# Two fused image blocks on one core: background work placed behind the even decay, finer steps for TensorE, and the first projection in two halves

## The chip, the cores and the metric

The kernel runs on one core of a Trainium2 chip. The metric is the device time of one execution in microseconds; the lower it is, the better. A time is the median of several runs; the profile is of one further execution.

The engines are TensorE (PE in the profile, its weight loads PEld), VectorE (DVE), ScalarE (ACT), GpSimd (POOL) and SyncE (SP), which issues all the DMAs of this kernel. Each engine works off its own list of instructions in order, and waits at an instruction until what that needs is there. SBUF is the memory that all of them work in, PSUM the smaller one that PE writes to; ACT and DVE use both.

## The reference

All arrays are float32. There are 16 images of 64 x 64 positions with 96 channels, and two layers, each added to its input (x + layer(norm(x))), where the norm is over groups of 3 channels of one image.

Layer 0 enlarges an image by Fourier interpolation, applies 96 -> 384 channels, a quadratic function, 384 -> 96 channels, a low-pass filter, and takes every second position. Layer 1 is a selective scan in four directions over the 4096 positions:

```python
xz = einsum('bhwc,pc->bhwp', x, in_proj_w);  xc, z = xz[..., :192], silu(xz[..., 192:])
xc = silu(depthwise_conv3x3(xc) + conv_b)              # 192 channels
xs = 4 orders of xc: by rows, by columns, and both reversed
dts, Bs, Cs = split(einsum('bkdl,kcd->bkcl', xs, x_proj_weight))     # 6, 16, 16
delta = softplus(einsum('bkrl,kdr->bkdl', dts, dt_projs_weight) + bias)
for t:  h = exp(delta_t * A) * h + (delta_t * u_t) * B_t;   y_t = sum_n h * C_t
y = sum of the four directions, put back in order;  layernorm over 192;  * z;  out_proj
```

For each image, direction, channel (192) and state (16) there is thus one recurrence over 4096 steps.

## The kernel before, in words

**Three kinds of work.** `front(mi)` (L240 to L517) makes of image mi the scan's inputs: layer 0, the second norm, the 3x3 convolution as nine matmuls ("taps", L482) and the gate z; it stores them to DRAM by rows (L473, L474) and, through the tile `col`, by columns (L508, L513). `scan()` (L615 on) does the recurrences of all images. `finish(mi)` (L519 to L608) adds the directions, applies norm, gate and output matrix, and stores the image. front and finish are generators: at each `yield` they hand back control, so that their instructions can be written into the scan's list in small steps. `front(0)` runs ahead of the scan, and `finish` of the last image behind it (L953 to L964).

**The scan.** An image has 8 steps (two pairs of directions, four stretches of T = 1024 positions each), a step has 6 blocks of 64 channel rows, a block 4 *units* of four states; 16 x 8 x 6 x 4 = 3072 units. Ahead of a step, `project` (L633 to L698) computes delta and delta * u ("dtu") for its 1024 positions in two halves of TB = 512, for three groups of channels each: a matmul (L666), six ACT instructions that make the softplus's parts e, m, w, d (L674 to L681), four matmuls with the identity that add them up (L686), a product on DVE (L691) and a copy on ACT (L692), and two stores to DRAM. The very first projection has nothing beside it (L738); the others are spread over the step before.

A unit has an odd half (e = 1) and an even half (e = 0), each of 128 partitions by 1024 positions. The loop L872 writes, in this order:

- `recur(n, 1)`: the odd scan on DVE (L770 or, backwards, L772), `keep` of its last value (L778), and ACT's `decay(n + 1, 1)`: exp(delta * A) for the next unit, L755. In every fifth unit (SHARE) the product with C follows on DVE (L906)
- `slot(0)`: the first background position
- POOL's product of the odd half with C (L915, not in every fifth unit), and `drive(n + 2)`: dtu * B, on POOL (L761)
- `recur(n, 0)`: the even scan on DVE; `read_out(n - 1)`: 16 matmuls (L794) that sum over the states
- `slot(1)`: the second background position (L923)
- the even half's product with C on DVE (L924), `keep` on ACT (L778), `decay(n + 1, 0)` on ACT (L755), and, once in a block, the copy of its result (L805)
- `slot(2)`: the third background position (L931); then loads of what comes: delta (L703), B and C rows (L722).

The decays write into the PSUM pool `sc_aps` (L629), which has two places of two banks each; the tile is called `da`. The odd scan reads its da and writes into the tile `b`; in every fifth unit, and always for the even half, the scan writes over da, and the product with C reads that. The program is written under a manual schedule (L953): the order on each engine is that of the code. Which of a pool's free places a tile gets is settled when the program is built.

**Background positions.** `slot` (L852) gives a step to the projection of the next step (`step_gen`, PSLICES = 71 steps over 72 positions), and one to `front` of the next image or, when that is through, to `finish` of the last one. An image has POS = 576 positions; a `Background` (L822) advances while its counted steps are behind SLICES / POS of the positions. A plain `yield` counts 1, `yield HEAVY` counts 2, and after `yield WAIT` the generator goes on only at a third position (L832).

**Memories.** Tiles of front and finish come from `b2p` (11 pieces of 128 x 512, L184), and from `b16` and `b18`, one large place each (L182, L183). In the scan the 8 PSUM banks are split into two for front and finish (`b_ps`), four for the decays, one for y and one for the projection (`gps`, L628 to L631).

Of the kernel before, what the change touches and what calls it, by code (L numbers as in the profile page):

```python
# [54 lines left out]
UPS = 100  # L55
# [16 lines left out]
SLICES = 550  # L72
# [7 lines left out]
def tile_two_blocks(  # L80
# [159 lines left out]
    def front(mi):  # L240
# [71 lines left out]
        o_last = None  # L312
        for p0 in range(0, UPS, PP):

            t1 = b18.tile([HW, PP, C], F32, name="t1", tag="b18")
            xr = fetch_x(0)
            for _ in range(3):
                yield
            for cg in range(3):
                u_ps = [bank([HW, 16, PP], "u_ps") for _ in range(2)]  # L320
                for k in range(16):
                    for a in range(2):
                        on = slice(64 * a, 64 * a + 64)
                        nc.tensor.matmul(
                            u_ps[a][:, k, :], lhsT=xr[k // 8][on, k % 8, :], rhs=up_s[on, p0:p0 + PP],
                            start=True, stop=True,
                        )
                    if k == 7:
                        yield
                if cg < 2:  # L330
                    xr = fetch_x(cg + 1)
                yield
                for a in range(2):
                    c0 = 48 * a + 16 * cg
                    nc.scalar.copy(t1[:, :, c0:c0 + 16], u_ps[a].rearrange("w c p -> w p c"))
                    yield
# [4 lines left out]
            for g in range(PP // PG):  # L341
# [8 lines left out]
                for j in range(HB + 1):  # L350
# [10 lines left out]
                    if j == 2 and sd is not None:  # L361
                        stow(sd, row - 2 * PG)
                    if j < HB:
                        h_ps[j] = bank([128, PG * UPS], "h_ps")
                        nc.tensor.matmul(  # L365
                            h_ps[j], lhsT=w1t_s[:, 128 * j:128 * (j + 1)],
                            rhs=xu.rearrange("c p q -> c (p q)"), start=True, stop=True,
                        )
                    elif g < PP // PG - 1:
                        xu_ps = widen(t1, g + 1)  # L370
# [90 lines left out]
        for i, n, tiles, both in ((0, 128, 8, 0), (1, 64, 4, 4)):  # L461
# [14 lines left out]
            for t in range(tiles):  # L476
                c_ps = bank([128, 8, HW], "c_ps")
                for tap in range(9):
# [8 lines left out]
                    if tap == 2 and turned is not None:  # L487
                        turn(*turned)
                    if tap % 3 == 2 and tap < 8:
                        yield HEAVY  # L490
# [13 lines left out]
                yield HEAVY  # L504
# [14 lines left out]
    def finish(mi):  # L519
# [19 lines left out]
        for t in range(8):  # L539
# [7 lines left out]
            for ob, n in ((0, 128), (1, 64)):  # L547
                oc = slice(128 * ob, 128 * ob + n)
                y_ps = bank([n, 8, HW], "yc")
                for i, (w, of) in enumerate(((pmat_s[:, 0, oc], y0), (pd_s[:, 0, oc], u0), (pd_s[:, 1, oc], yu))):  # L550
                    nc.tensor.matmul(  # L551
                        y_ps, lhsT=w, rhs=of.rearrange("c (h w) -> c h w", w=HW), start=(i == 0), stop=False
                    )
                if tail is not None:
                    tail = next(tail, None) and tail
# [3 lines left out]
                yield HEAVY  # L559
# [18 lines left out]
            yield HEAVY  # L578
# [5 lines left out]
            yield HEAVY  # L584
# [30 lines left out]
    def scan():  # L615


        with ExitStack() as es:
# [9 lines left out]
            banks.append(es.enter_context(tc.tile_pool(name="b_ps", bufs=2, space=PSUM)))  # L628
            aps = es.enter_context(tc.tile_pool(name="sc_aps", bufs=2, space=PSUM))  # L629
            yps = es.enter_context(tc.tile_pool(name="sc_yps", bufs=1, space=PSUM))  # L630
            gps = es.enter_context(tc.tile_pool(name="sc_gps", bufs=1, space=PSUM))  # L631

            def project(mi, pair, lc, out):  # L633
# [3 lines left out]
                out["rows"] = rows = dctx.tile([2, 2 * NS, T], F32, name="rows")  # L637
                out["delta"] = [dctx.tile([128, T], F32, name=f"delta_d{v}") for v in range(3)]
                out["dtu"] = [dctx.tile([128, T], F32, name=f"dtu_d{v}") for v in range(3)]
                xs_d = image[mi]["xs"]  # L640
                order = (0, 2, 1)

                def fetch_u(v, t):
                    uv = up_.tile([128, TB], F32, name="u")
# [3 lines left out]
                ahead_u = [fetch_u(v, 0) for v in order]  # L648
                for _ in range(4):
                    yield  # L650
                for t in range(0, T, TB):
                    u, ahead_u = dict(zip(order, ahead_u)), []
                    pp = gps.tile([128, TB], F32, name="pp", tag="g")
# [4 lines left out]
                    pr = pj.tile([128, TB], F32, name="pr")  # L658
# [3 lines left out]
                    for i, v in enumerate(order):  # L662
                        if i == 0:
                            yield
                        s = gps.tile([128, TB], F32, name="s", tag="g")
# [7 lines left out]
                        e, d, m, w = (pj.tile([128, TB], F32, name=k) for k in ("e", "d", "m", "w"))  # L673
# [9 lines left out]
                        s = gps.tile([128, TB], F32, name="s", tag="g")  # L683
# [3 lines left out]
                        for _ in range(3):  # L687
                            yield
                        dtu = pj.tile([128, TB], F32, name="dtu")
                        delta = pj.tile([128, TB], F32, name="delta")  # L690
# [6 lines left out]
                        if t + TB < T and i < 2:  # L697
                            ahead_u += [fetch_u(k, t + TB) for k in (order[:1], order[1:])[i]]  # L698
# [39 lines left out]
            for _ in project(*steps[0], ctxs[0]):  # L738
                pass
            bc = {(what, 0, j): fetch_bc(ctxs[0], 0, j, what) for j in range(NQ) for what in range(2)}  # L740
            dtus = {0: fetch_dtu(ctxs[0], 0)}
            deltas = {(0, e): fetch_delta(ctxs[0], 0, e) for e in (1, 0)}
# [114 lines left out]
            def next_step(st, mi):  # L857

                nonlocal step_gen
                if st < len(steps):  # L860
                    if steps[st][0] > mi:
                        ahead_gen.drain()
                    step_gen = Background(project(*steps[st], ctxs[st]), PSLICES, 3 * per_step)
# [8 lines left out]
            for n, (st, bi, j) in enumerate(units):  # L872
# [50 lines left out]
                slot(1)  # L923
# [4 lines left out]
                if n >= 1 and units[n - 1][2] == NQ - 1:  # L928
                    storing = store(n - 1)
                    next(storing)  # L930
                slot(2)  # L931
# [128 lines left out]
```

## Time and profile before

| | us |
|---|---|
| median of 3 runs | 21514.79 |
| lowest and highest of them | 21493.7 and 21515.12 |
| the profiled execution's own time | 21508.85 |
| its span in the profile | 21507.1 |
| first product of POOL (the loop begins) | 530.5 |
| last store of the scan issued (the loop ends) | 21347 |
| busy in the span: DVE, POOL | 19512.2, 19511.8 |
| busy in the span: PE, ACT | 16918.9, 13741.5 |

The granted clock of PE was 0.856 over the span. In the groups, a line gives source line, engine, operation, tiles (out<-in), shapes and count, then the busy time, the mean of one in ns, and the idle time of the engine just before them with what ended it. In the waits, "A <- B" means that A's engine stood still until B was done: total us, times, longest. In the timeline: start and duration in us, and in brackets the idle time ahead. A float32 matmul stands in the trace as two.

### The profile page before, as it was taken

The numbers are of one execution on the slowest core, as the hardware profiler recorded it, in microseconds if no ns is written. First come the engines' busy times: TensorE is split into PE (matmuls) and PEld (weight loads), VectorE is DVE, ScalarE is ACT, GpSimd is POOL, SyncE is SP. The second block draws the span as 40 slices with busy tenths as digits, with TensorE's granted clock in tenths as the row PEclk, the third lists the DMA queues.
The fourth block names the chain that finished last, engine by engine and source line by source line (L and its number), as shares of the span: only waits on it lengthen the run. The fifth ranks groups of instructions, "written<-read, shape, count | busy, mean of one in ns | idle before, by whom it ended". The sixth has DMA issues, their size and how long they took to land. (4 is left out here: it accounts for less than half of the span.)

```text
span 21507.1 us, 273615 instructions
## 1 busy us (share of the span) xinstructions
PE 16918.9 (79%) x98988; PEld 7271.3 (34%) x98988; DVE 19512.2 (91%) x12983; ACT 13741.5 (64%) x20546; POOL 19511.8 (91%) x5538
## 2 busy tenths in 40 slices
PE   7776877878878788787878778788787888878855
PEld 4423324233332333324333242333423333243221
DVE  0999999999999999999999999999999999999997
ACT  3666666667666666666666666676666666666553
POOL 0999999999999999999999999999999999999996
PEclk8887888888889888898888888888898888888877
DMA  2565565656656566565655656566565665656654
GB/s 74 180 207 184 199 224 187 217 192 204 217 189 227 187 218 203 187 228 183 219 197 200 224 191 215 192 208 215 185 227 187 211 203 192 230 184 217 222 186 140
DMA packets 1855466, 4277.13 MB, mean 199 GB/s; under 512 B 449438, under 2 KB 548670, under 8 KB 1852062
## 3 DMA queue, kind: packets, MB, share of 16 engines
q1 hardware_dynamic: 1854110, 4259.62, 58.8%
q8 instruction: 781, 12.80, 0.2%
q14 instruction: 575, 4.71, 0.1%
HBM read 3380.58 MB, written 878.18 MB: 198 GB/s over the span
## 5 line engine op out<-in xcount | busy, mean ns | idle before, releaser
L761 POOL TENSOR_TENSOR b<-dtu,bt 128x2048 f32<-128x2048 f32 x3072 | 13905.1, 4536 | 594.2 <-DMA dtu<-dtu_d 530.5
L755 ACT ACTIVATE da<-delta,a_s 128x1024 f32<-128x1024 f32 x6144 | 6852.3, 1116 | 2859.4 <-DVE b L924 888.2
L915 POOL TENSOR_TENSOR b<-b,ct 128x1024 f32<-128x1024 f32 x2458 | 5804.1, 2361 | 1235.6 <-DVE new L778 832.6
L794 PE MATMUL y<-b,fold_s 128*32 128x256 f32 x49152 | 3837.1, 435 | 1111.6 <-DVE b L924 551.4
L924 DVE TENSOR_TENSOR b<-da,ct 128x1024 f32<-128x1024 f32 x3072 | 3756.5, 1223 | 93.9
L770 DVE TENSOR_TENSOR_SCAN da<-da,new,b 128x1024 f32<-128x1024 f32 x1383 | 3246.5, 2347 | 282.8 <-ACT da L755 274.7
L772 DVE TENSOR_TENSOR_SCAN da<-da,new,b 128x1024 f32<-128x1024 f32 x1382 | 3242.4, 2346 | 125.5 <-ACT da L755 119.1
L794 PEld LDWEIGHTS y<-b,fold_s 128*32 128x32 f32 x49152 | 1392.0, 119 | 3857.0 <-issue 1333.0
L778 ACT COPY new<-da 128x1 f32<-128x1 f32 x2764 | 434.6, 157 | 2786.4 <-DVE b L924 2294.7
L772 DVE TENSOR_TENSOR_SCAN b<-da,new,b 128x1024 f32<-128x1024 f32 x922 | 2157.9, 2341 | 47.0 <-ACT da L755 46.1
L770 DVE TENSOR_TENSOR_SCAN b<-da,new,b 128x1024 f32<-128x1024 f32 x921 | 2156.6, 2342 | 41.1 <-ACT da L755 39.5
L482 PE MATMUL c_ps<-xgp,wtap_s 96*128 96x512 f32 (+1 forms) x4608 | 1721.3, 642 | 203.6 <-ACT row L500 199.1
L686 PE MATMUL s<-w,ident_s 128*128 128x512 f32 x1536 | 1175.4, 857 | 872.0 <-ACT w L681 752.3
L666 PE MATMUL s<-pr,dtw_s 128*128 128x512 f32 x1536 | 939.0, 696 | 544.6 <-ACT delta L692 328.0
L365 PE MATMUL h_ps<-xu,w1t_s 96*128 96x500 f32 x1920 | 1059.4, 652 | 306.7 <-ACT hsq L348 124.2
L377 PE MATMUL o_ps<-w2c_s,hsq 128*100 128x96 f32 x9600 | 1031.9, 266 | 170.0 <-ACT hsq L348 143.7
L772 DVE TENSOR_TENSOR_SCAN da<-da,b 128x1024 f32<-128x1024 f32 x461 | 1055.9, 2291 | 118.4 <-ACT da L755 116.7
L770 DVE TENSOR_TENSOR_SCAN da<-da,b 128x1024 f32<-128x1024 f32 x460 | 1053.4, 2290 | 106.5 <-ACT da L755 104.3
L377 PEld LDWEIGHTS o_ps<-w2c_s,hsq 128*100 128x100 f32 x9600 | 966.1, 178 | 357.2 <-ACT hsq L348 184.9
L686 PE MATMUL s<-e,ident_s 128*128 128x512 f32 x1536 | 1022.9, 755 | 0.0
L482 PEld LDWEIGHTS c_ps<-xgp,wtap_s 96*128 96x128 f32 (+1 forms) x4608 | 600.1, 172 | 1154.9 <-issue 873.0
L787 PE MATMUL y<-y,ident_s 128*128 128x512 f32 x768 | 534.1, 784 | 538.6 <-ACT yt L805 537.1
(128 smaller groups left out, 21920.7 us busy)
## 6 DMA issues: line engine op xcount, KB each, us to landing
dtu<-dtu_d SPq DMA_DIRECT2D x1536, 512.0 KB
delta<-delta_d SPq DMA_DIRECT2D x1536, 512.0 KB
bt<-rows SPq DMA_DIRECT2D x1024, 512.0 KB
ct<-rows SPq DMA_DIRECT2D x1024, 512.0 KB
u<-xs_d SPq DMA_DIRECT2D x896, 256.0 KB
dtu_d<-dtu SPq DMA_DIRECT2D x768, 256.0 KB
delta_d<-delta SPq DMA_DIRECT2D x768, 256.0 KB
xr<-in_x SPq DMA_DIRECT2D x768, 128.0 KB
```

The source lines that it names most:

```text
L365: nc.tensor.matmul(h_ps[j], lhsT=w1t_s[:, 128 * j:128 * (j + 1)], rhs=xu.rearrange("c p q -> c (p q)"), start=True, stop=True,)
L377: nc.tensor.matmul(o_ps[:, p, :], lhsT=hsq[j][:, UPS * p:UPS * (p + 1)], rhs=w2c_s[:, j, :], start=(j == 0), stop=(j == HB - 1),)
L482: nc.tensor.matmul(c_ps[p:p + n], lhsT=wtap_s[:, tap, 128 * i:128 * i + n], rhs=xgp[:, h0:h0 + 8, dx:dx + HW], start=(tap == 0), stop=(tap ...
L666: nc.tensor.matmul(s, lhsT=dtw_s[:, pair, v, :], rhs=pr, start=True, stop=True)
L686: nc.tensor.matmul(s, lhsT=ident_s, rhs=of, start=(k == 0), stop=(k == 3))
L755: nc.scalar.activation(da, deltas[n // NQ, e], AF.Exp, scale=a_s[:, k, g, units[n][2]:units[n][2] + 1])
L761: nc.gpsimd.tensor_mul(b, dtus[n // NQ], bt.unsqueeze(1).to_broadcast([128, 2, T]))
L770: nc.vector.tensor_tensor_scan(out, da, b, before, ALU.mult, ALU.add)
L772: nc.vector.tensor_tensor_scan(out[:, ::-1], da[:, ::-1], b[:, ::-1], before, ALU.mult, ALU.add)
L794: nc.tensor.matmul(y[32 * q:32 * q + 32, e, :], lhsT=fold_s, rhs=b[:, e, QT * q:QT * q + QT], start=(pair == 0 and j == 0 and e == 0), sto ...
L915: nc.gpsimd.tensor_mul(h, h, bc[1, r, j])
L924: nc.vector.tensor_mul(bs[n][:, 0, :], h, bc[1, r, j])
```

## The change

Four things change.

1. **The second background position** moves from ahead of the even half's product L924 to behind `keep`, the even decay and the start of `store`, directly ahead of the third position.
2. **Smaller steps.** The convolution yields after every second tap instead of every third, and counts 1, not 2; in the projection the four identity matmuls are split two and two; in finish a matmul group is split and most steps count 1. The convolution takes the 64-channel part first and the 128-channel part second. SLICES goes from 550 to 499.
3. **Earlier x loads** in front: the first two groups of the next quarter are fetched during the last group of the one before, and each group is asked for one ahead.
4. **The first projection** runs as two generators, one for each half, taken in turn. The second half uses the large places b16 and b18, both use a pool of four PSUM banks, and the scan's PSUM pools are opened after it. Once the first channel group of both halves is stored, the first rows of B, the first dtu and the first two deltas are fetched.

```diff
-SLICES = 550
+SLICES = 499
...
-            xr = fetch_x(0)
-            for _ in range(3):
-                yield
+            if not asked:
+                asked += [fetch_x(0), fetch_x(1)]
+                for _ in range(3):
+                    yield
             for cg in range(3):
+                xr = asked.pop(0)
...
-                if cg < 2:
-                    xr = fetch_x(cg + 1)
+                if cg == 0:
+                    asked.append(fetch_x(2))
...
+                    if j >= 2 and g == PP // PG - 1 and p0 + PP < UPS:
+                        asked.append(fetch_x(j - 2))
...
-        for i, n, tiles, both in ((0, 128, 8, 0), (1, 64, 4, 4)):
+        for i, n, tiles, both in ((1, 64, 4, 4), (0, 128, 8, 0)):
...
-                    if tap == 2 and turned is not None:
+                    if tap == 3 and turned is not None:
                         turn(*turned)
-                    if tap % 3 == 2 and tap < 8:
-                        yield HEAVY
+                    if tap % 2 == 1:
+                        yield
...
                         for k, of in enumerate((w, e, d, m)):
                             nc.tensor.matmul(s, lhsT=ident_s, rhs=of, start=(k == 0), stop=(k == 3))
-                        for _ in range(3):
+                            if k == 1:
+                                yield
+                        for _ in range(2):
                             yield
...
-            for _ in project(*steps[0], ctxs[0]):
-                pass
-            bc = {(what, 0, j): fetch_bc(ctxs[0], 0, j, what) for j in range(NQ) for what in range(2)}
-            dtus = {0: fetch_dtu(ctxs[0], 0)}
-            deltas = {(0, e): fetch_delta(ctxs[0], 0, e) for e in (1, 0)}
+            bc, dtus, deltas = {}, {}, {}
+            far_u = b16.tile([128, 4, TB], F32, name="far_u", tag="b16")
+            far_w = b18.tile([128, 6, TB], F32, name="far_w", tag="b18")
...
+            with tc.tile_pool(name="side_ps", bufs=4, space=PSUM) as side:
+                todo = [project(*steps[0], ctxs[0], side, 0), project(*steps[0], ctxs[0], side, TB, far.get)]
+                while todo:
+                    todo = [g for g in todo if next(g, todo) is not todo]
+                    if ctxs[0]["made"] >= 2 and not dtus:
+                        bc[0, 0, 0] = fetch_bc(ctxs[0], 0, 0, 0)
+                        dtus[0] = fetch_dtu(ctxs[0], 0)
+                        for e in (1, 0):
+                            deltas[0, e] = fetch_delta(ctxs[0], 0, e)
+            for j in range(NQ):
+                for what in range(2):
+                    if (what, 0, j) not in bc:
+                        bc[what, 0, j] = fetch_bc(ctxs[0], 0, j, what)
...
                 recur(n, 0, h)
                 if n >= 1:
                     read_out(n - 1)
-                slot(1)
                 nc.vector.tensor_mul(bs[n][:, 0, :], h, bc[1, r, j])
                 keep(n, 0, h, nc.scalar.copy)
                 if n < last:
                     decay(n + 1, 0)
                 if n >= 1 and units[n - 1][2] == NQ - 1:
                     storing = store(n - 1)
                     next(storing)
+                slot(1)
                 slot(2)
```

## The prediction

> **What bounds the kernel.** I read the profile in this order: the page's groups, busy time in windows, VectorE's waits, then a timeline of one unit. A unit is one pass of the loop L872; each has an odd half (e = 1) and an even half (e = 0). From the groups (instructions, busy us, mean ns, idle time before):
>
> ```profile
> L761 POOL TENSOR_TENSOR b<-dtu,bt 128x2048 f32<-128x2048 f32 x3072 | 13905.1, 4536 | 594.2 <-DMA dtu<-dtu_d 530.5 <-PE y L794 47.9 <-issue 12.3
> L755 ACT ACTIVATE da<-delta,a_s 128x1024 f32<-128x1024 f32 x6144 | 6852.3, 1116 | 2859.4 <-DVE b L924 888.2 <-DVE b L772 771.1 <-DVE b L770 710.8
> L915 POOL TENSOR_TENSOR b<-b,ct 128x1024 f32<-128x1024 f32 x2458 | 5804.1, 2361 | 1235.6 <-DVE new L778 832.6 <-issue 233.9 <-DVE b L770 59.1
> ```
>
> The loop runs from about 530 to 21345 us. The window view of that stretch (length, then busy us of PE, PEld, DVE, ACT, POOL):
>
> ```profile
> 530.00:21345.00 20815.00, 16385.12 (x96414) 6995.96 (x96414) 19484.51 (x12916) 13505.68 (x20168) 19511.35 (x5530) 0.86 0.60 203
> ```
>
> POOL and DVE are both busy 94% of it, with some 1300 us idle each. Who waits for whom? POOL's idle time stands ahead of L915, mostly for DVE; DVE's waits (total us, times, longest) are these:
>
> ```profile
> DVE dtu L691 <- PE s L686: 430.6, 135, 134.9
> DVE da L770 <- ACT da L755: 379.0, 366, 3.4
> ...
> DVE da L772 <- ACT da L755: 235.8, 240, 4.0
> DVE b L772 <- ACT da L755: 177.6, 88, 4.7
> ...
> DVE b L770 <- ACT da L755: 72.6, 58, 22.0
> ...
> DVE da L770 <- POOL b L761: 8.7, 17, 0.9
> ```
>
> DVE hardly waits for POOL (8.7 us here, 23 us over all scans); it waits for ScalarE's decays: 865 us in all, of which 843 are inside the loop's steady part (the 22.0 is the first scan). So DVE sets the pace, and what it waits for is the decay. Why is the decay late? One unit on ACT, then on DVE (start us, duration):
>
> ```profile
> 17888.10 0.16 ACT L778 COPY new<-da 128x1 f32<-128x1 f32 x1
> 17890.35 1.12 ACT L755 ACTIVATE da<-delta,a_s 128x1024 f32<-128x1024 f32 x1 [2.09 <-DVE b L770]
> 17891.40 0.58 ACT L692 COPY delta<-s 128x512 f32<-128x512 f32 x1
> ```
> ```profile
> 17886.23 1.23 DVE L924 TENSOR_TENSOR b<-da,ct 128x1024 f32<-128x1024 f32 x1
> 17887.38 0.68 DVE L691 TENSOR_TENSOR dtu<-s,u 128x512 f32<-128x512 f32 x1
> 17887.97 2.34 DVE L770 TENSOR_TENSOR_SCAN b<-da,new,b 128x1024 f32<-128x1024 f32 x1
> 17890.35 0.15 DVE L778 COPY new<-b 128x1 f32<-128x1 f32 x1
> 17891.50 2.36 DVE L770 TENSOR_TENSOR_SCAN da<-da,new,b 128x1024 f32<-128x1024 f32 x1 [1.00 <-ACT da L755]
> ```
>
> The even decay of the next unit could run at 17888.3, behind the copy L778; its old place was read for the last time by L924, done at 17887.46. It starts at 17890.35 instead, as the *odd* scan ends, and the even scan follows 1.00 us late. Not ACT work delays it but its place in PSUM: the pool sc_aps has two, and this tile was given the one that the same unit's odd decay had just filled. The places are fixed when the program is built, by an order of all engines' instructions that the builder assumes, so they can be read off the program. In before, 477 of 3071 even decays take the odd tile's place. I matched them with the scans of the trace: all 477 even scans waited, 479 us together; the other 2593 waited 59 us together. Odd scans waited 305 us. That is the 843.
>
> **The change, part by part.**
>
> *Position behind the even decay (L923 to behind L930).* No instruction is added or removed. On ACT, the second position's work goes behind the copy L778 and the even decay; its dtu, yz and other products on DVE go behind the product L924; its DMAs keep their order on SP ahead of the third position's. In the builder's order the even decay comes earlier, and in the changed program 184 even decays take the odd tile's place, not 477. So 293 waits go, each 479 / 477 = 1.00 us: **-293 us**. Is all of it won? What is late next is POOL: per five units it needs 5 x 4.536 + 4 x 2.361 = 32.1 us, against 20801 / 3071 x 5 = 33.9 us now, so 1.8 us per five units could go before POOL alone sets the pace, and 293 us are 0.48. From the other side, a line through the times of the loop's 612 groups of five units over their number of such decays gives 1.6 us each, which would be 470 us; heavy stretches have more of them, so I don't take that. Half (POOL in the way in some stretches) to 470 are my ends; I take 293, the wait's own length.
>
> *The cost of the same move.* ACT's other work in the loop is 13505.7 - 6852.3 (L755) - 434.6 (L778) - 443.8 (L805) = 5775 us, 0.63 us per position. The second position's share used to fill ACT's wait for L924 (2294.7 us ahead of L778); now it stands between the even decay and the next odd decay, and queued behind it are the third position's work, the odd decay and then DVE's odd scan. Spare time there: the odd decay can start when the odd scan has ended and has until L770 (2.35) and L924 (1.22) are done, 3.57 - 1.12 = 2.45 us. I went through the trace's units and put each one's second-position work into that room: where it only shifts what did not fit ACT's idle time, odd scans wait 102 us more; if nothing is absorbed, 279 us. Against it stands that 293 times ACT no longer sits idle for two microseconds with this work behind it, and the next item. Ends -100 and +279; I take **+40**.
>
> *Smaller parts for TensorE* (two taps per step, four products of L686 split two and two, yields in finish; SLICES 499). Matmuls, their order within each generator and their number stay; they change places with read_out's by a position. The steps count less: front 389 weighted steps become 368, finish 142 become 126, and 499 for 550 spreads them over the same units: front ends at unit 141 of 192 (135), finish at 190 (185), so nothing is drained in a burst. The rows this can touch are L691's waits in the loop (430.6 less the first projection's six, 134.9 and some 60.7, = 235 us) and ACT's waits for PE inside late odd decays. Now the last two products of a group are issued a position later, with dtu where it was, but most dtu have a unit (6.8 us) against some 5.5 us of products. Ends: -150 to +100; I take **0**, its gain being in the +40. The x fetches moved ahead: PE waited 61.7 us for xr over the whole run, hidden in the loop by DVE; in the head some 7 us. The 12 of them pass SP's stores earlier, with the same number of instructions; I count **-4** in the head.
>
> *First projection in halves.* Head before: last conv instruction at 424.5, then
>
> ```profile
> 515.25 0.56 SPq L722 DMA_DIRECT2D bt<-rows  x1
> ```
> ```profile
> 531.51 8.95 POOL L761 TENSOR_TENSOR b<-dtu,bt 128x2048 f32<-128x2048 f32 x2 [530.50 <-DMA dtu<-dtu_d]
> 533.97 2.15 ACT L755 ACTIVATE da<-delta,a_s 128x1024 f32<-128x1024 f32 x2 [19.11 <-DMA delta<-delta_d]
> ...
> 536.23 2.29 DVE L770 TENSOR_TENSOR_SCAN b<-da,b 128x1024 f32<-128x1024 f32 x1 [21.99 <-ACT da L755]
> ```
>
> Six chains run one behind the other from 439.1 to 514.9, two of them about 24 us. Two interleaved: 1.13 (L666) + 5.8 (ACT until the first chain's w; one chain is 3.57) + 2 x 6.4 (L686 of both) = 19.7. Three pairs save 13 us, the second half's first products 1: -14. The first dtu, deltas and bt are fetched after the first pair, so from the end of the projection to the first scan the 21 us shrink to about 5 (two decays, 2.15, and the second bt behind ct on SP): -16. Replacing eight stores of the last column by four is within 2 us. Head with the -4: **-34 us**, ends -20 and -55 (PE busy in that stretch is 52.8 of 81.5 us, so the projection can't lose more than 29).
>
> The page "TensorE: Matmul & The Clock Gate" of the Trainium skill (Part 1) says PE's clock is halved until it has been busy for some 3.4 us. The rows of 424 to 520 us go that way: the products of w, e, d, m take 1121, 1016, 832, 610 ns in that order within a group. By the rule, two groups in a row would run the second at the last rate, some 6 us less than my sum; nothing here depends on it.
>
> **Sum.** The profiled execution took 21508.85 us (span 21507.1), 6 us below the median of 21514.79. -293 + 40 + 0 - 34 = -287: 21508.85 - 287 = **21222 us**. The tail after 21345 (160 us) keeps its order.
>
> **Rivals.**
> - *POOL takes over.* For: at 17883 to 17895 POOL stands without a gap while DVE waits its 1.00. Against: POOL idles 1300 us in the loop. If only a third of the waits becomes time, -100 + 40 - 34: 21415.
> - *The odd decays pay (slower).* Place: ACT between even decay and next odd decay, above all where a row of the convolution adds 0.69 + 0.59 + 2 x 1.28 (table loads) = 3.85 us at the third position, over the 2.45 of spare. If the second position's 0.63 us lands on the path in a third of the units, 1024 x 0.63 = 645: -293 + 645 - 34 = 21827; it decides from 327 us, 0.11 us per unit.
> - *More than the waits*: each late decay costs 1.6 us, and shorter PE parts take 100 us of the odd waits: -470 - 60 - 34: 20945.
> - *The places do not matter* (something else holds the scan by then): only the head, 21475, counted with the first rival.
>
> **Chances.** Forecast (21050 to 21330) 0.66; POOL takes over 0.15 (a fifth of it within 0.2%); odd decays pay 0.12 (0.04 within 0.2%, 0.07 slower, the rest a small gain); more 0.07. The range takes the forecast and most of the first rival: 21040 to 21430. 0.2% is 43 us, about what a measurement of this kernel can tell from no change. Faster 0.86, same 0.07, slower 0.07.
>
> **What would show it.** In the changed profile: waits of "da" scans for L755 near 620 - 293 = 330 us; POOL's wait for L778 down by some 250; first POOL product of a second drive near 500, first scan near 502. Wrong: "b" scans waiting over 450 us for L755 (odd decays), or scans waiting over 150 us for POOL's L761, or a timeline where an even decay in its own place still starts late.

## The result, and the profile after

The changed kernel takes **21998.9 us** (median of 4 runs, 21993.24 to 22015.79) against 21505.53 (4 runs, 21493.7 to 21515.12): ratio **1.0231**, 95% interval 1.0213 to 1.0249. It was forecast at 21222, 287 us below the profiled execution before, and is 493 us slower. The profiled execution took 21993.24 us, span 21991.5.

Lines of code have moved: the decay is L788 (L755 before), drive L794 (L761), the scans L803 and L805 (L770, L772), keep L811 (L778), POOL's and DVE's product with C L948 and L956 (L915, L924), read_out L827 (L794), w L691 (L681), the identity products L696 (L686), dtu L702 (L691), and finish's products yz L577 and L587 (L570, L580). First the groups, as before:

```profile
L794 POOL TENSOR_TENSOR b<-dtu,bt 128x2048 f32<-128x2048 f32 x3072 | 13897.7, 4532 | 586.5 <-DMA dtu<-dtu_d 474.2
L788 ACT ACTIVATE da<-delta,a_s 128x1024 f32<-128x1024 f32 x6144 | 6856.3, 1116 | 2900.1 <-DVE b L956 1199.1
L948 POOL TENSOR_TENSOR b<-b,ct 128x1024 f32<-128x1024 f32 x2458 | 5798.5, 2359 | 1721.8 <-DVE new L811 1061.5
...
L811 ACT COPY new<-da 128x1 f32<-128x1 f32 x2764 | 434.1, 157 | 3523.7 <-DVE b L956 3045.9
```

The busy time of these lines is as before to 0.1%. POOL's wait for DVE grew to 1061.5 us (forecast: 250 less), and ACT's wait at keep for the product with C grew from 2294.7 to 3045.9. The loop's window:

```profile
494.00:21833.00 21339.00, 16609.35 (x96414) 7012.05 (x96414) 19434.74 (x12916) 13530.95 (x20167) 19513.27 (x5529) 0.85 0.60 198
```

It is 524 us longer, with DVE and POOL as busy as before (19484.51 and 19511.35). From first to last scan it is 21332.6 us for 20805.8, and DVE's idle time there 1899.1 for 1322.5. DVE's waits:

```profile
DVE dtu L702 <- PE s L696: 910.6, 380, 142.7
...
DVE b L805 <- ACT da L788: 180.9, 93, 4.9
DVE da L803 <- ACT da L788: 175.2, 179, 3.2
DVE yz L577 <- ACT sq L565: 166.4, 60, 27.9
DVE da L805 <- ACT da L788: 144.9, 82, 4.9
DVE yz L587 <- ACT sq L583: 104.7, 51, 3.9
DVE b L805 <- ACT new L811: 76.3, 54, 3.7
...
DVE b L803 <- ACT da L788: 33.4, 29, 3.5
```

Scans that write over da (the even ones, and every fifth odd one) wait 320 us for ACT's decay, where it was 615 and the forecast 330: the waits that were to go did go. In their place **dtu waits for the identity products**, 739 us inside the loop for 235 (the rest of the 910.6 is the first projection), and finish's yz for ACT's squares, 162 us in the loop for about nothing. The odd scans wait 375 us for ACT, for 306. Of these, the profile puts 100 us down to keep (`ACT new`, 76 of them at `b L805`), which ended last; but in 68 of these 69 cases the odd decay that the scan reads had itself ended less than 0.3 us before, with keep right behind it. They are late odd decays too.

One dtu on PE and DVE, in the same unit (1183) before and after. Before:

```profile
8568.93 2.08 PE L686 MATMUL s<-w,ident_s 128*128 128x512 f32 x2
8570.80 1.30 PE L686 MATMUL s<-e,ident_s 128*128 128x512 f32 x2
8571.93 1.02 PE L686 MATMUL s<-d,ident_s 128*128 128x512 f32 x2
8572.79 1.02 PE L686 MATMUL s<-m,ident_s 128*128 128x512 f32 x2
```
```profile
8574.07 1.22 DVE L924 TENSOR_TENSOR b<-da,ct 128x1024 f32<-128x1024 f32 x1
8575.21 0.68 DVE L691 TENSOR_TENSOR dtu<-s,u 128x512 f32<-128x512 f32 x1
```

After:

```profile
8726.85 2.07 PE L696 MATMUL s<-w,ident_s 128*128 128x512 f32 x2
8728.71 1.92 PE L696 MATMUL s<-e,ident_s 128*128 128x512 f32 x2
8730.56 1.91 PE L327 MATMUL u_ps<-up_s,xr 64*64 64x25 f32 x32
8732.39 2.07 PE L696 MATMUL s<-d,ident_s 128*128 128x512 f32 x2
8734.26 1.82 PE L696 MATMUL s<-m,ident_s 128*128 128x512 f32 x2
```
```profile
8729.51 1.22 DVE L956 TENSOR_TENSOR b<-da,ct 128x1024 f32<-128x1024 f32 x1
8736.12 0.69 DVE L702 TENSOR_TENSOR dtu<-s,u 128x512 f32<-128x512 f32 x1 [5.39 <-PE s L696]
```

Two things are seen. The products start 3.9 us before DVE is free (at 8730.73), not 6.3 (8575.21): the *lead* is shorter. And a step of front (L327) now stands between the second and third product, so that the group takes 9.2 us for 4.9. DVE, in order, stands 5.39 us, and the next scan behind it.

The head did what was forecast, and a little more:

```profile
458.65 0.57 SPq L734 DMA_DIRECT2D bt<-rows  x1
...
467.28 4.51 POOL L794 TENSOR_TENSOR b<-dtu,bt 128x2048 f32<-128x2048 f32 x1 [466.27 <-DMA dtu<-dtu_d]
491.70 2.15 ACT L788 ACTIVATE da<-delta,a_s 128x1024 f32<-128x1024 f32 x2
...
494.36 2.29 DVE L803 TENSOR_TENSOR_SCAN b<-da,b 128x1024 f32<-128x1024 f32 x1 [3.31 <-ACT da L788]
```

The first scan starts at 494.4 (forecast 502; before 536.2).

### The profile page after: what moved, and what is told of

It reads as the page before. It is cut to its first block, busy times and chain, and to the rows that moved or that the text cites. A ratio compares the mean times of both kernels' runs of the same rounds, so it can differ in the third digit from the quotient of the medians.

```text
span 21991.5 us, 273276 instructions
## 1 busy us (share of the span) xinstructions
PE 17134.9 (78%) x98988; PEld 7282.7 (33%) x98988; DVE 19462.4 (88%) x12983; ACT 13767.8 (63%) x20546; POOL 19518.3 (89%) x5538
## 5 line engine op out<-in xcount | busy, mean ns | idle before, releaser
L794 POOL TENSOR_TENSOR b<-dtu,bt 128x2048 f32<-128x2048 f32 x3072 | 13897.7, 4532 | 586.5 <-DMA dtu<-dtu_d 474.2
L788 ACT ACTIVATE da<-delta,a_s 128x1024 f32<-128x1024 f32 x6144 | 6856.3, 1116 | 2900.1 <-DVE b L956 1199.1
L948 POOL TENSOR_TENSOR b<-b,ct 128x1024 f32<-128x1024 f32 x2458 | 5798.5, 2359 | 1721.8 <-DVE new L811 1061.5
L827 PE MATMUL y<-b,fold_s 128*32 128x256 f32 x49152 | 3888.6, 442 | 809.9 <-DVE b L956 514.9
L956 DVE TENSOR_TENSOR b<-da,ct 128x1024 f32<-128x1024 f32 x3072 | 3762.6, 1225 | 105.7
L803 DVE TENSOR_TENSOR_SCAN da<-da,new,b 128x1024 f32<-128x1024 f32 x1383 | 3246.0, 2347 | 136.3 <-ACT da L788 134.7
L805 DVE TENSOR_TENSOR_SCAN da<-da,new,b 128x1024 f32<-128x1024 f32 x1382 | 3241.7, 2346 | 134.1 <-ACT da L788 114.9
L811 ACT COPY new<-da 128x1 f32<-128x1 f32 x2764 | 434.1, 157 | 3523.7 <-DVE b L956 3045.9
L827 PEld LDWEIGHTS y<-b,fold_s 128*32 128x32 f32 x49152 | 1422.6, 121 | 3598.3 <-issue 1540.8
L805 DVE TENSOR_TENSOR_SCAN b<-da,new,b 128x1024 f32<-128x1024 f32 x922 | 2158.6, 2341 | 182.5 <-ACT da L788 134.4
L696 PE MATMUL s<-w,ident_s 128*128 128x512 f32 x1530 | 1225.8, 894 | 1280.8 <-ACT w L691 1141.0
L803 DVE TENSOR_TENSOR_SCAN b<-da,new,b 128x1024 f32<-128x1024 f32 x921 | 2156.4, 2341 | 2.5 <-ACT da L788 2.5
L487 PE MATMUL c_ps<-xgp,wtap_s 96*64 96x512 f32 (+1 forms) x4608 | 1730.4, 627 | 234.1 <-ACT row L505 228.7
L702 DVE TENSOR_TENSOR dtu<-s,u 128x512 f32<-128x512 f32 x765 | 525.2, 687 | 920.6 <-PE s L696 910.6
L805 DVE TENSOR_TENSOR_SCAN da<-da,b 128x1024 f32<-128x1024 f32 x461 | 1055.1, 2289 | 39.3 <-ACT da L788 30.0
L803 DVE TENSOR_TENSOR_SCAN da<-da,b 128x1024 f32<-128x1024 f32 x460 | 1052.8, 2289 | 40.5 <-ACT da L788 40.5
L696 PE MATMUL s<-e,ident_s 128*128 128x512 f32 x1530 | 1071.3, 792 | 0.0
L487 PEld LDWEIGHTS c_ps<-xgp,wtap_s 96*64 96x64 f32 (+1 forms) x4608 | 588.5, 169 | 1195.1 <-issue 845.9
```

What stands on the lines that cost most here:

```text
L487: nc.tensor.matmul(c_ps[p:p + n], lhsT=wtap_s[:, tap, 128 * i:128 * i + n], rhs=xgp[:, h0:h0 + 8, dx:dx + HW], start=(tap == 0), stop=(tap ...
L696: nc.tensor.matmul(s, lhsT=ident_s, rhs=of, start=(k == 0), stop=(k == 3))
L788: nc.scalar.activation(da, deltas[n // NQ, e], AF.Exp, scale=a_s[:, k, g, units[n][2]:units[n][2] + 1])
L794: nc.gpsimd.tensor_mul(b, dtus[n // NQ], bt.unsqueeze(1).to_broadcast([128, 2, T]))
L803: nc.vector.tensor_tensor_scan(out, da, b, before, ALU.mult, ALU.add)
L805: nc.vector.tensor_tensor_scan(out[:, ::-1], da[:, ::-1], b[:, ::-1], before, ALU.mult, ALU.add)
```

## The experiments

Two theories stood at first. **A**: the split products cost, since the last two come one position later with dtu where it was. **B**: the moved position costs, through the order on ScalarE. Times are medians of 4 runs or more (9 or 10 for b_split, b_halves and b_places_pos) with the profiled one, each beside the kernel before on the same chip (21499 to 21507 us); ratios with 95% intervals. An interval is some 30 us to either side, so a difference of two kernels is good to about 45.

| kernel | us | ratio (interval) |
|---|---|---|
| b_pos | 21629.22 | 1.0056 (1.0041 to 1.0071) |
| b_split | 21456.57 | 0.9975 (0.9966 to 0.9985) |
| b_places | 20958.76 | 0.9747 (0.9732 to 0.9761) |
| b_halves | 21459.54 | 0.9980 (0.9970 to 0.9990) |
| b_places_pos | 21477.80 | 0.9989 (0.9979 to 0.9998) |
| b_places_mid | 21055.97 | 0.9789 (0.9774 to 0.9803) |
| a_unpos | 21734.06 | 1.0109 (1.0093 to 1.0126) |
| a_unsplit | 21762.70 | 1.0123 (1.0108 to 1.0139) |
| b_halves_places | 20930.14 | 0.9733 (0.9718 to 0.9747) |
| b_halves_places_split | 21055.57 | 0.9793 (0.9779 to 0.9808) |
| b_places_gens | 21338.05 | 0.9923 (0.9906 to 0.9940) |
| a_places | 21740.75 | 1.0111 (1.0096 to 1.0126) |
| g_noorder | 21172.65 | 0.9847 (0.9833 to 0.9862) |
| g_notaps | 21011.00 | 0.9771 (0.9756 to 0.9786) |
| g_nofin | 21134.83 | 0.9832 (0.9815 to 0.9848) |
| b_places_order | 20979.86 | 0.9757 (0.9743 to 0.9772) |
| g_sl515 | 21254.90 | 0.9887 (0.9871 to 0.9904) |
| b_places_taps | 21094.65 | 0.9814 (0.9799 to 0.9829) |

### One part alone on the kernel before

**b_pos**: the position moved, nothing else (part 1 of the change).

> Before, with the second background position behind the even decay and nothing else; 153 even decays take the odd tile's place (477 in before). Theory A (the split of the four identity products is what makes dtu late): the waits of dtu for TensorE stay near 235 us, the even scans' waits fall by some 325 us, the time falls by 200 to 320 us. Theory B (ScalarE's parts of the projection, now behind the even decay, make the identity products and with them dtu late): dtu waits rise by 300 us or more, L686's wait for L681 rises from 752 us to over 1050, and the time is no lower than before.

It is slower by 0.56%, although only 153 even decays take the odd tile's place in it. PE's wait at the identity products for w is 1181 us for 752, as theory B had it; but inside the loop dtu waits 382 us for 235, about half the rise that it named. The odd scans' waits for ACT rise as much, from 306 us to 454, which neither theory named.

**b_split**: only the identity products split, as in the change.

> Before, with the four identity products of the projection issued two and two, one position apart, and nothing else; 387 even decays take the odd tile's place. Theory A: the last two stand on TensorE behind a step of front that waits for ScalarE; dtu waits for TensorE rise from 235 us to over 550 and the time rises by 200 to 400 us. Theory B: dtu waits stay within 100 us of 235, and the time falls by up to 90 us (90 fewer borrowed places).

Slightly faster, so A alone is not the cause, though dtu waits 386 us in the loop for 235. But the builder gave 387 even decays the borrowed place, not 477, so two things changed.

**b_places**: each half gets its own place, which takes the builder's choice out of the comparison.

```diff
-aps = ...(tc.tile_pool(name="sc_aps", bufs=2, space=PSUM))
+aps = ...(tc.tile_pool(name="sc_aps", bufs=1, space=PSUM))
...
-da = aps.tile([128, T], F32, name="da")
+da = aps.tile([128, T], F32, name="da", tag=f"da{e}")
```

> Before, with a place of its own for the odd and for the even decay in PSUM (a tag for each, one buffer each), and nothing else. If each wait of an even scan on a borrowed place is time on the path: 477 waits of 1.00 us go, the time falls by 350 to 480 us, to about 21070. If another wait (POOL, or dtu) takes their place: the even scans' waits fall just so, but the time falls by less than 200 us.

549 us faster, 1.15 us for each of the 477 places, and more than forecast. In the loop the even scans' waits for ACT fall by 358 us (538 to 180), the odd scans' by 85, dtu's by 56; so a place costs more than the even scan's own wait. POOL's wait for DVE falls from 832.6 to 473.2:

```profile
L915 POOL TENSOR_TENSOR b<-b,ct 128x1024 f32<-128x1024 f32 x2458 | 5804.7, 2362 | 709.0 <-DVE new L778 473.2 <-issue 80.7 <-DVE b L770 48.4
```

DVE sets the pace and POOL follows; no wait takes the place of the one removed.

**b_halves**: only the first projection in halves.

> Before, with the first projection in two interleaved halves and its early fetches, and nothing else. The first scan starts near 494 us instead of 536, as in the changed kernel; the loop keeps its length. Time 42 us lower, within 15. If the early start is lost to POOL, whose second drive waits for the second rows of B: 25 to 30 us.

48 us faster, first scan at 497.9. The head's part of the change is a gain.

### The move, with the places out of the way

**b_places_pos**: own places and the moved position. **b_places_mid**: own places, the second position behind DVE's product L924 but ahead of keep and the even decay, so that DVE's order is that of the change and ACT's that of before.

```diff
                 nc.vector.tensor_mul(bs[n][:, 0, :], h, bc[1, r, j])
+                slot(1)
                 keep(n, 0, h, nc.scalar.copy)
```

> The kernel with own places (20959 us), with the second background position behind the even decay: the move alone, since no decay borrows a place in either. Theory B (the move itself costs, by ScalarE's background work behind the even decay): 21300 to 21450, some 450 us above, with L686's wait for L681 from 697 to over 1000 us and dtu's waits from 180 to over 350 us. Theory of the prediction (the move itself costs 40 us or less, and the loss is elsewhere): 20920 to 21000.

> The kernel with own places, with the second background position behind the even half's product on VectorE but still ahead of the copy and the even decay: VectorE's order is that of the changed kernel, ScalarE's that of before. Theory B (ScalarE's order is what costs): 20959 within 80 us. Theory C (VectorE's order costs, with dtu and its like directly ahead of the odd scan): 21250 or more, as with the full move.

The move costs **519 us** (21477.80 - 20958.76) with DVE's and ACT's order both changed, 97 with DVE's alone (theory B had 80 at most for the second, and 490 for the first). So some 420 come from ACT's order. Waits of PE and DVE in b_places:

```profile
PE s L686 <- ACT w L681: 696.6, 322, 15.7
```
```profile
DVE dtu L691 <- PE s L686: 375.6, 105, 135.4
DVE b L772 <- ACT da L755: 128.1, 84, 3.2
DVE b L770 <- ACT da L755: 58.9, 49, 22.6
```

of b_places_pos:

```profile
PE s L686 <- ACT w L681: 1131.7, 350, 18.1
```
```profile
DVE dtu L691 <- PE s L686: 577.1, 247, 133.5
DVE b L770 <- ACT da L755: 151.1, 105, 22.2
DVE b L772 <- ACT da L755: 115.6, 56, 4.6
DVE b L772 <- ACT new L778: 65.1, 33, 3.8
DVE b L770 <- ACT new L778: 26.0, 24, 2.3
```

and of b_places_mid:

```profile
PE s L686 <- ACT w L681: 687.3, 324, 16.1
```
```profile
DVE dtu L691 <- PE s L686: 323.5, 79, 135.5
```

So the move is paid in two places, about equally. In the loop dtu waits 383 us for 179, and all odd scans (every fifth among them) wait 440 us for ACT's odd decay, or for the keep behind it, for 221. The even scans gain 120 us, small products of finish and norm lose 130.

I matched every dtu in the traces with its products. Lead is the mean time from the start of the first product to DVE being free for dtu, at the four of the six places of a step where dtu itself does not move (at the other two, units 4 and 15, dtu stands in the second position); late is how many dtu of the 126 at each place waited:

| kernel | lead, us (units 1, 7, 12, 18 of 24) | late |
|---|---|---|
| b_places | 8.0, 6.7, 7.0, 4.9 | 0, 4, 15, 45 |
| b_places_mid | 8.0, 6.4, 7.2, 5.0 | 1, 7, 10, 47 |
| b_places_pos | 5.6, 5.4, 5.3, 3.5 | 45, 29, 28, 90 |
| b_halves_places_split | 8.0, 6.5, 7.0, 4.9 | 14, 13, 25, 60 |
| after | 5.6, 5.3, 5.8, 4.6 | 96, 63, 85, 63 |

The move takes 1.3 to 2.4 us of lead. ACT now stands idle at keep (2717.0 us for 2366.2) with the second position's work behind it in its queue, then works off both positions' in one bunch behind the even decay; w comes late, PE waits for it with everything behind it, and dtu, whose place in DVE's list has not changed at these four, finds its sum not there. The odd decay stands behind the same bunch, and the odd scan finds it not there.

### One part put back in the changed kernel

**a_unpos**: the position as before. **a_unsplit**: the four products together as before.

> The changed kernel with the second position put back ahead of the even half's product; 464 even decays borrow a place (184 in the changed kernel). Theory B: faster than the changed kernel although 280 more places are borrowed: 21300 to 21500; dtu's waits from 739 us to under 450, the waits of finish's products from 160 us to under 40. If the smaller parts and the split carry the loss by themselves: 22100 or more.

> The changed kernel with the four identity products issued together again; 190 even decays borrow a place (184). If the split is harmful only beside the moved position (its last two products then come out behind the read-out and the step of front that the moved position brings): dtu's waits fall from 739 us to about 400, the time to 21650 to 21750. If the split has no part in the loss: 22000 within 60 us.

a_unpos is 265 us faster than the changed kernel, though 464 even decays borrow their place in it for 184. But it is still 230 us above the kernel before: a miss, as the move was to be nearly all. Something else among the finer steps costs. a_unsplit gains 236: beside the move, the split costs that much (dtu waits 332 us in the loop for 739). Its odd scans wait 560 us for ACT, for 375 in the changed kernel.

### Each part with own places

**b_halves_places**: places and halves. **b_halves_places_split**: the same with the split. **b_places_gens**: own places and the finer steps of front and finish (part 2 without the split, and part 3). **a_places**: the changed kernel with own places.

> The kernel before with two parts: places of their own for odd and even decay in PSUM (alone 0.9747) and the first projection in two halves (alone 0.998). They touch different stretches (the loop, and the head), so the theory that they add gives 20959 - 48 = 20911 us, ratio 0.972 to 0.973; a rival, in which the head's gain is eaten because the first units then wait for something else (rows of C, the later deltas), gives 20959. First scan near 498 us.

> The first kernel of this set plus the split of the four identity products two and two. Theory (the split makes dtu late by one position in any case: the kernel before with the split alone had 386 us of dtu waits for 235, and what it seemed to win came from 90 fewer borrowed places): slower than without it by 50 to 150 us, 20960 to 21060. Rival (the split costs only when the second position lies behind the even decay): within 40 us of 20911.

> The kernel before with places of their own for odd and even decay, plus only the finer steps of front and finish (convolution two taps a step, its 64-channel part first, finish in lighter steps, x loads earlier, SLICES 499); the position, the identity products and the head as before. Theory (the finer steps cost by themselves, as the changed kernel with its position put back suggests: 21734 with the head's 48 and the split's some 50 gained): 21200 to 21300 us, against 20959 with the places alone, and it shows in the units that carry the convolution's 128-channel part. Rival (they cost only where the decays share their places, or beside the split products): within 50 us of 20959.

> The changed kernel with places of their own for odd and even decay. 184 even decays took the odd one's place in it; at the 1.15 us each that the kernel before gained, 184 x 1.15 = 212, so 21787 us, ratio 1.013. Rival: the even scans' waits are hidden by now behind the late dtu and the late odd decays, so nothing: 21990. The waits of dtu for the identity products stay near 740 us under both, and the waits of the odd scans too.

**b_halves_places has the lowest time of this study**, 20930.14 us. The halves add 29 us to the gain of the places, for 48 alone; two kernels so close can't be told apart here. In its loop DVE is busy 95.8% of the time:

```profile
494.00:20770.00 20276.00, 16179.05 (x96414) 6892.23 (x96414) 19426.51 (x12916) 13529.22 (x20168) 19500.51 (x5529) 0.87 0.62 208
```

The split costs 125 us: theory A holds in part, once the places no longer hide it. The lead is as it was (table), but the group takes longer (6.6 us for 4.9 in the mean at unit 1), and dtu waits 369 us in the loop for 181. The scans then wait 119 us less for ACT, so that this path nets some 70 us; another 72 are in the rows of one tiny product, L236 (last section). The finer steps cost **379 us**, taken as nothing in the prediction. a_places is 258 us below the changed kernel, 1.40 us for each of 184 places, more than the 212 expected.

### Which of the finer steps

The next six have own places. From b_places_gens, **g_noorder** puts the order of the convolution's parts back, **g_notaps** its three taps a step with HEAVY (SLICES 511), **g_nofin** finish's steps (SLICES 515), and **g_sl515** changes SLICES alone. On b_places, **b_places_order** and **b_places_taps** (SLICES 538) do one edit alone.

```diff
 g_notaps, and reversed in b_places_taps
-                    if tap == 3 and turned is not None:
+                    if tap == 2 and turned is not None:
                         turn(*turned)
-                    if tap % 2 == 1:
-                        yield
+                    if tap % 3 == 2 and tap < 8:
+                        yield HEAVY
...
                 turned = t, row, z
-                yield
+                yield HEAVY
```

> The kernel with own places and all finer steps (21338 us), with one part of the finer steps put back: the convolution takes its 128-channel part first again. Theory O (the order is what costs: eight dense tiles of rows, gates and table loads now lie beside the backward stretches in units 120 to 152, where the scans wait 443 us against 78): back to 20960 to 21050. Theory T (the finer taps cost, wherever the tiles lie): 21300 or more.

> The same kernel (21338 us) with the convolution's steps of before put back (three taps a step, counting 2; SLICES 511 so that front and finish end at the same units). Theory T (the lighter count packs a tile's row, gate and table loads into fewer units, 1.9 for 2.1 a tile, and they then meet the decays more often): 20990 to 21100. Theory O: 21300 or more.

> The same kernel (21338 us) with finish's steps of before put back (SLICES 515). Units 144 to 192, where finish runs, take 1.6 us x 8 x 16 = 200 us more in all than with the places alone; if that comes from finish's lighter steps, 21140 to 21200; if it is front running later into that stretch (its end moves from unit 135 to 141), 21300 or more.

> The kernel before with places of their own (20959 us) and one more edit: the convolution takes its 64-channel part first. Theory O: 21200 to 21330, most of the 379 us that all finer steps cost. Theory T: within 60 us of 20959.

> The kernel with own places and all finer steps (21338 us), only SLICES raised from 499 to 515, so that the same steps come 3% faster. Putting finish's steps back brought 21135 us, but with SLICES 515. Theory P (pace: where the steps fall against the units decides, and the same steps at another pace lose less): 21130 to 21220. Theory F (finish's lighter steps themselves cost): 21290 or more.

> The kernel before with places of their own (20959 us) and one more edit: the convolution's two taps a step with the lighter count, SLICES 538 so that front and finish end where they did. Undoing the taps in the kernel with all finer steps won 327 of its 379 us. Theory T (taps by themselves): 21200 to 21290. Theory I (the finer steps cost together, not each by itself, as the order of the convolution did: 21 us alone, 165 when undone): 20960 to 21080.

Undone in the kernel with all of them, the taps give back 327 us, the order 165, finish's steps with the pace 203, of which the pace alone gives 83. Alone, the taps cost 136 and the order 21. g_notaps lands where theory T had it, but g_noorder and b_places_taps do not: neither O nor T holds by itself, P and F each explain a part, and the last run comes out between T and I, just above I. The taps cost most, and more than twice as much beside the rest. The earlier x loads were in all of these and were not tried apart. The waits of b_places_gens:

```profile
DVE da L779 <- ACT da L762: 270.5, 169, 5.2
DVE b L779 <- ACT da L762: 205.1, 114, 4.9
```

and of g_notaps:

```profile
DVE da L779 <- ACT da L762: 169.0, 100, 6.0
DVE b L779 <- ACT da L762: 144.7, 102, 3.9
```

L779 are the backward scans, beside which the convolution runs; with the places alone they wait 93.6 + 128.1 = 222 us. (Over all scans, forward ones too, the waits for ACT in the loop rise by 191 us.) The same tiles' matmuls, ACT work and table loads stand there in other positions. Over the whole run ACT's `e` waits for the projection's matmul 165 us with all finer steps, 86 with the places alone, 34 without the taps. Which single instruction makes the decay late was not settled.

## Why the prediction was wrong

**What was right.** DVE sets the pace, and an even decay in the borrowed place costs it: own places bring 549 us. The term of -293 held: the even scans' waits for ACT fell by 282 us (538 to 256); and by times, the sharing costs 258 us in the changed kernel (21998.9 - 21740.75) and 547 in the one before (21505.53 - 20958.76), so the move to fewer of them is worth -288. That the times meet the term so closely is partly luck: one place is worth 1.15 us in the kernel before and 1.40 in the changed one, both between the 1.00 that I took and the 1.6 of the line through groups of five units. The head gave -42 by the traces (forecast -34), -48 alone, -29 beside own places. POOL did not take over: scans wait about 11 us for it.

**The step that failed first** is the cost of the move on ScalarE, "+40" with ends of -100 and +279: it is **+519** with own places. I had priced the second position's work only as something that may shift the *odd decay*, against the spare time ahead of the odd scan, and even credited an ACT that "no longer sits idle for two microseconds with this work behind it". It sits there longer, 3045.9 us for 2294.7. With own places the odd scans wait 219 us more (221 to 440), mis-sized but inside my ends. What the term left out is that the work is itself on a path: w, behind which PE waits in order, then dtu, behind which DVE waits in order: 204 us more. I had L691 in the list of waits (235 us in the loop) and did not ask who makes it late. Finish's and norm's small products, 130 us, were not in the term either.

**The second** is "Smaller parts for TensorE", taken as 0 with ends of -150 and +100. The reason given was that "most dtu have a unit (6.8 us) against some 5.5 us of products". That was the lead of a group issued in one piece: split, the last two products queue behind front's step (1.91 us in the unit shown), and beside the move the lead itself is 4.6 to 5.8. It is +125 for the split and +379 for the finer steps. Of the latter, 191 us are the scans' waits for ACT's decays and 71 the rows of L236; why the decays come late stays open. That front ends at unit 141 for 135, with nothing drained in a burst, was no measure of where the steps fall within a unit.

**The account**, by medians: halves -29, move +519, split +125, finer steps +379, all with own places; together 213 less than their sum, probably since the same waits are hit twice; sharing of places 258 - 547 = -288 (rounded). That is +493.

**The rivals.** The slower one, "the odd decays pay", gave 21827 and named the right engine, the right stretch of ACT's list and half of the move's mechanism: b_pos and b_places_pos show late odd scans, 454 and 440 us. In the changed kernel its mark, odd scans waiting over 450 us for L755, does not appear: they wait 375. There the toll is collected at dtu and yz, and none of my marks for "wrong" named them. A dtu that is late gives the decay of the scan behind it time to end; without the split, where dtu waits less, the odd scans wait 560 us (a_unsplit). That the one wait hides the other is the likely reading; no run was made for it alone.

The late group also ran slowly. The granted clock (third column from the end) in the stretches of the unit shown:

```profile
8725.00:8729.00 4.00, 3.98 (x33) 2.90 (x34) 2.97 (x3) 2.18 (x3) 4.00 (x2) 0.50 0.93 303
8729.00:8733.00 4.00, 4.00 (x35) 2.33 (x35) 1.70 (x2) 0.51 (x2) 4.00 (x2) 0.50 0.52 209
8733.00:8736.00 3.00, 3.00 (x4) 0.67 (x2) 0.00 (x0) 1.57 (x3) 1.97 (x1) 0.52 0.00 0
8736.00:8740.00 4.00, 4.00 (x45) 2.25 (x45) 3.85 (x3) 0.59 (x1) 2.74 (x1) 1.00 0.48 158
```

PE is busy throughout from 8725 on, yet stays at half clock for 11 us. In the kernel before the same group went over to 0.94 in the stretch from 8571 to 8574, some 6 us after PE's last idle time (4.49 us, to 8565.16). The page "TensorE: Matmul & The Clock Gate" of the Trainium skill (Part 1) gives some 3.4 us of sustained work for that; by these rows it can take longer. By the starts in the unit's rows, the four products take 7.4 us for 4.9 before, and L327 in between 1.8; what each is worth of the 5.39 us was not tried apart.

## What to carry to other kernels

Background work that looks free on one engine can be the first link of a chain through two other in-order queues: follow each of its results to the instruction that reads it, and measure the lead between them before moving either. Then look at what stands behind it in its own queue; here both cost about the same. And where a wait that was expected does not show, see whether another one ahead of it on the same engine hides it. A step split for one engine's sake lengthens the group for whoever waits for its last part, by all that is queued in between. And where the builder may give a tile the place that was just filled, give the two tiles places of their own first; here that one edit is worth more than all others, and without it every other comparison is mixed up with it.

## What the runs showed of the hardware

A busy row can hold a wait. DVE's product of 96 x 1 numbers at L236 takes 155 ns at the least, but in b_places_gens:

```profile
L236 DVE TENSOR_TENSOR nb<-nmean,rg x32: 155/5718/12333, 38.7 to 19314.9; 96x1 f32<-96x1 f32 x32
```

(min, median, max in ns). One of them, and what POOL did meanwhile:

```profile
2480.61 12.32 DVE L236 TENSOR_TENSOR nb<-nmean,rg 96x1 f32<-96x1 f32 x1 [0.23 <-ACT rg L233]
```
```profile
2483.98 8.94 POOL L768 TENSOR_TENSOR b<-dtu,bt 128x2048 f32<-128x2048 f32 x2
```

POOL ran without a gap from 2477.18 on. The row ends at 2492.93, POOL's products at 2492.92. It is so in all 30 cases in the loop of b_places_gens: the row, 2.6 us or longer, ends 13 to 18 ns after a product of POOL, while its operand rg was ready before it began (it starts 31 ns or more after `rg` ended). In the changed kernel 24 of the 30 take 0.30 us or less; at 20 of these POOL stood idle when the row began, and at the other four its product was almost through. So by these rows this product on DVE stands until POOL has finished the product under way, and those that follow it without a gap, and the profile counts that time as busy. The busy time of such a row is not work.

The 30 rows count 192 us as busy in b_places_gens, 121 in b_places, 28 in the changed kernel. They move with where norm's steps happen to fall against POOL, and, in the profiled executions, they enter the differences above: 71 us of the finer steps' 379, 72 of the split's 125 (120 to 192), 38 of the 97 of b_places_mid. No run took them out.
